# Joining the last weighted-sum burst of a cross-attention batch to the first burst of the next batch

## The chip, the cores and the metric

The kernel runs on one core of one Trainium2 chip. The metric is the device time of one execution in microseconds (us), as the median of several runs. The engines are named as the profile names them: PE (TensorE, matmuls; PEld is its weight loads), DVE (VectorE), ACT (ScalarE), POOL (GpSimd) and SP (SyncE, which issues most DMAs).

## The reference, cut to what matters

A decoder of two layers over 32 batches of 100 tokens with 256 features, all in float32. Each layer has self-attention, cross-attention over a context of 361 rows and a feed-forward part (layer 0: a scaled ternary matmul; layer 1: eight experts, of which each token takes one). A residual sum and a layer norm follow each of the three. The change is in cross-attention, which for each batch and each of 16 heads is:

```
scores = q @ k.T                     # 100 x 361; layer 0 adds -log(distance)*|scale|
attn   = softmax(scores, axis=-1)
out    = attn @ v                    # 100 x 16 per head
y      = out.reshape(100, 256) @ Wo + bo
x      = layernorm(x + y)
```

## The kernel before

**Tiling.** Heads are taken in four groups of four (`NG = 4`). For a cross group, PE makes the scores of four heads in four PSUM banks (`score`, L277, a tile of which there is one, shared with self-attention). DVE then reads each head once, adds the bias and finds the row maximum (L360, "reads" below); POOL subtracts the maximum (L364, "subtractions"); PE turns the 100x361 weights in three chunks of 120 or so (`turn`, L374, four transposes a chunk); ACT takes the exponential out of PSUM into the tile `pT` (L375); and PE multiplies by the values (`sums`, L389). The values carry 16 columns of ones beside each head's 16, so the sums give the softmax's denominator too. Four heads share the array, each in its own 32 columns. A float32 matmul is two matmul instructions, so the profile counts twice what the code issues.

**Bursts.** `sums` does nothing for group 0; for group 1 it does groups 0 and 1 in one burst (48 instructions in the profile), for groups 2 and 3 one group each (24). ACT copies a burst out to `av_x` (L391). `pT` has two buffers, the values `v_cross` two.

**The order of the work** is written out by hand. Work is planned in slots, five a batch, each with places -1 to 3; `run_slots` issues a slot so: the scores of the step two slots ahead and the first two reads; places -1 and 0; the other reads; then for the step one slot ahead the three chunks of transposes, with places 1, 2 and 3 after them; and last the bursts of the slot's own step. Every engine has one queue in this order. The batch at slot `start` has its cross groups at `start + 0, 1, 3, 4`; the self step of the batch four later has the slot between (`start + 2`). So in the steady state a period of five slots is, named by slot modulo 5:

- slot 0: scores of a self step; it ends when the scores of group 2 start
- slot 1: scores of group 2, the transposes of the self step, the burst of groups 0 and 1
- slot 2: scores of group 3, the transposes of group 2
- slot 3: scores of the next batch's group 0, transposes of group 3, the burst of group 2 and that of the self step
- slot 4: scores of the next batch's group 1, transposes of its group 0, the burst of group 3

For the self step, DVE reads the 16 heads' scores twice, for the maximum (L318, tile `mx_s`) and for the subtraction (L321, `pr_s`).

**The batch's tail** follows from `start + 5`: `add_share` on POOL (L296, tile `y_x`); `normalised` (four PE transposes, L287, tile `r_n_x`; DVE L289 and L291, `o_x`); `transpose_rows` (L242, `r_x_ox`); `residual` (PE L303, `r_o_x`; DVE L304, L85, L87; POOL L89 and L90, `rs_x`); the centring (DVE L94). Layer 0 goes on with the next norm's statistics (`mv_n`, POOL `rs_n`), `feed_forward_input` (DVE L579 to L581, tile `xn`) and its transposes (`r_x_n`). Layer 1 goes on with transposes for the router (`r_x_m`), the router's logits (`r_l`), and per four batches the ranking of tokens (`r_p`) and sending of rows. Self-attention has the same tail with tiles ending in `_s`.

Of the kernel before, what the change touches and what calls it, by code (L numbers as in the profile page):

```python
# [10 lines left out]
F32 = mybir.dt.float32  # L11
# [5 lines left out]
B, S, D, H, DH = 32, 100, 256, 16, 16  # L17
SK = 361
E = 8
P = 128  # L20
NC2 = D // P
NG = 4
KCH = [(0, 120), (120, 120), (240, 122)]
# [21 lines left out]
SHARED = ("l0s_wq", "l0s_wk", "l0s_wv", "l0x_wk", "l0x_wv", "l0x_wq", "l0s_wo", "l0x_wo")  # L45
# [5 lines left out]
def head(g, j):  # L51

    return 8 * (g // 2) + 2 * j + g % 2
# [11 lines left out]
def decoder_kernel(ctx: ExitStack, tc: tile.TileContext, a: dict, out: bass.AP):  # L65
    nc = tc.nc
# [6 lines left out]
    xnT = state.tile([P, NC2, B, S], F32, name="xnT")  # L73
# [22 lines left out]
    with ExitStack() as att:  # L96
        w1 = att.enter_context(tc.tile_pool(name="w1", bufs=1))
        w2 = att.enter_context(tc.tile_pool(name="w2", bufs=2))
# [5 lines left out]
        def bank(tag):  # L104
            return ps_r.tile([P, 512], F32, tag="r", name=f"r_{tag}")

        def split(t, n):
            return t.rearrange("p (n s) -> p n s", n=n)
# [18 lines left out]
        c = {}  # L127
# [12 lines left out]
        shared = const.tile([P, E, NC2 * D], F32, name="shared")  # L140
# [62 lines left out]
              ("s", 1): masked(1.0 / 16.0, None, "qm_s1"), ("x", 1): masked(0.25, c["l1x_bq"], "qm_x1")}  # L203

        def spread_value_bias(n):
            wide = c[n + "_wide"] = w1.tile([P, NC2, P], F32, tag=f"fold_{n[2]}", name=f"fold_{n}")
            nc.vector.tensor_copy(wide, c[n + "_bv"].unsqueeze(2).to_broadcast([P, NC2, P]))

        def fold_value_bias(n):
# [22 lines left out]
        def next_tile(tiles):  # L232
            tiles.append(tiles.pop(0))
            return tiles[-1]

        live = {}
# [37 lines left out]
        def score(dst, qz, kT, g, j):  # L274
            k, p = divmod(g, 2)
            rows = slice(32 * j, 32 * j + 32)
            nc.tensor.matmul(dst, lhsT=qz[rows, p, k, :], rhs=kT[rows, k, :], start=True, stop=True)  # L277

        def score_banks(tag):
            return ps_s.tile([P, NG, 512], F32, tag="s", name=f"sc_{tag}")  # L280

        def normalised(avs, tag):


            psn = bank(f"n_{tag}")[:S].rearrange("p (h r) -> p h r", r=32)
            for g in range(NG):
                nc.tensor.transpose(psn[:, g * NG:(g + 1) * NG, :].rearrange("p h r -> p (h r)"), avs[:, g, :], ident)  # L287
            rc = sm.tile([S, H], F32, tag="rc", name=f"rc_{tag}")
            nc.vector.reciprocal(rc, psn[:, :, DH])  # L289
            o = w2.tile([S, H, DH], F32, tag="o", name=f"o_{tag}")  # L290
            nc.vector.tensor_tensor(o, psn[:, :, :DH], rc.unsqueeze(2).to_broadcast([S, H, DH]), ALU.mult)  # L291
            return o

        def add_share(share, kind, b, tag):
            y = w2.tile([S, D], F32, tag=f"y_{kind}", name=f"y_{kind}{tag}")
            nc.gpsimd.tensor_tensor(y, xs[b], share[:S], ALU.add)  # L296
            return y
# [9 lines left out]
        def self_step(l, b):  # L307
# [34 lines left out]

            return Step(scores, turn, sums)

        def cross_step(l, b, g):

            t, tag = live[l, b], f"x{l}_{b}_{g}"

            def scores():
                sc = score_banks(tag)[:S, :, :SK]  # L350
                for j in range(NG):
                    score(sc[:, j, :], t["qz_x"], t["kT_x"], g, j)
                pr = t["pr_x", g] = next_tile(pr_cross)
                bias = zero if l else t["bias"]
                alone = b >= B - 4

                def centre(j):
                    def do():
                        mx = sm.tile([S, 1], F32, tag="mxx", name=f"mx_{tag}_{j}")
                        nc.vector.tensor_tensor_reduce(pr[:, j, :SK], sc[:, j, :], bias, 1.0, LOWEST, ALU.add, ALU.max, mx)  # L360
                        if alone and j == NG - 1:
                            nc.vector.tensor_scalar(pr[:, j, :SK], pr[:, j, :SK], mx, None, ALU.subtract)
                        else:
                            nc.gpsimd.tensor_tensor(pr[:, j, :SK], pr[:, j, :SK], mx.to_broadcast([S, SK]), ALU.subtract)  # L364
                    return do
                return [centre(j) for j in range(NG)]

            def turn(i):
                k0, n = KCH[i]
                if i == 0:  # L370
                    t["pT_x", g] = w2.tile([P, len(KCH), NG, S], F32, tag="pT", name=f"pT_{tag}")
                pt = split(bank(f"t_{tag}_{i}")[:, :NG * S], NG)
                for j in range(NG):
                    nc.tensor.transpose(pt[:n, j, :], t["pr_x", g][:, j, k0:k0 + n], ident[:S, :S])  # L374
                nc.scalar.activation(t["pT_x", g][:n, i], pt[:n], AF.Exp)  # L375

            def sums():

                if g == 0:
                    return  # L380
                groups = (0, 1) if g == 1 else (g,)
                if g == 1:
                    t["av_x"] = w2.tile([P, NG, S], F32, tag="avs_x", name=f"avs_{tag}")
                av = split(bank(f"a_{tag}")[:, :len(groups) * S], len(groups))
                for h, part in enumerate(groups):
                    for i, (k0, n) in enumerate(KCH):
                        n = min(n, SK - k0)
                        for j in range(NG):
                            nc.tensor.matmul(av[32 * j:32 * j + 32, h, :], lhsT=t["v_x"][:n, i, head(part, j), :],  # L389
                                             rhs=t["pT_x", part][:n, i, j, :], start=(i == 0), stop=(i == len(KCH) - 1))  # L390
                nc.scalar.copy(t["av_x"][:, groups[0]:g + 1, :], av)  # L391

            return Step(scores, turn, sums)

        plan, steps, bursts = {}, {}, {}

        def at(slot, place, do):
            plan.setdefault((slot, place), []).append(do)
# [68 lines left out]
        def starts(l, b):  # L467


            return LAYER[l] + SLOTS * b, LAYER[l] + (2 * b - 10 if b < 4 else SLOTS * (b - 4) + 2)  # L470
# [59 lines left out]
        def plan_batch(l, b):  # L530
            start, early = starts(l, b)
            t = live[l, b] = {}
            sx = f"l{l}x"
            tag = f"{l}_{b}"

            def keep(key, f):
                def do():
                    t[key] = f()
                return do
# [34 lines left out]
                nc.sync.dma_start(t["v_x"].rearrange("p i h r -> p (i h r)"), values_dram[b - AHEAD[0]])  # L574

            def feed_forward_input():
                xn = t["xn"] = w2.tile([S, D], F32, tag="xn", name=f"xn_{b}")
                mean, rs = t["ln_n"]
                nc.vector.scalar_tensor_tensor(xn, xs[b], mean, c["ffn_g"][:S], ALU.subtract, ALU.mult)  # L579
                nc.vector.scalar_tensor_tensor(xn, xn, rs, c["ffn_b"][:S], ALU.mult, ALU.add)  # L580
                nc.vector.tensor_reduce(absmax[:S, b:b + 1], xn, AX.X, ALU.max, apply_absolute_value=True)  # L581
# [43 lines left out]
            for g in range(NG):  # L625
                slot = start + (0, 1, 3, 4)[g]
                steps[slot] = cross_step(l, b, g)
                bursts.setdefault(slot, []).append(steps[slot].sums)
            at(start + 5, 0, keep("y_x", lambda: add_share(c[sx + "_bo"], "x", b, tag)))
            at(start + 5, 2, keep("o_x", lambda: normalised(t["av_x"], f"x{tag}")))  # L630
            at(start + 6, 0, keep("oT_x", lambda: transpose_rows(flat(t["o_x"]), "ox", tag)))
# [7 lines left out]
            else:  # L639
                at(start + 9, 0, keep("x3T", lambda: transpose_rows(xs[b], "m", tag)))  # L640
                first, n = group_of(b)
                r, steps_of_group = ROUTING[max(0, b - (B - 3))]
                at(start + r[0], r[1], router)
                if b == first + n - 1:
                    for do, (s, place) in zip((ranked, exponentials, ahead_of, counted, shares, rows_of), steps_of_group):
                        at(start + s, place, lambda do=do: do(first, n))
                    s, place = steps_of_group[-1]
# [11 lines left out]
        def group_of(b):  # L659

            if b >= B - 2:
                return b, 1
            first = b // GROUP * GROUP
            return first, min(GROUP, B - 2 - first)
# [145 lines left out]

        at(-16, 1, load_soon)
        at(-16, 1, lambda: spread_value_bias("l0s"))
        at(-16, 1, lambda: spread_value_bias("l0x"))
        at(SLOTS * B + 2, 0, lambda: spread_value_bias("l1x"))
        at(-12, 3, fold_first)
        at(-8, 1, lambda: fold_value_bias("l0x"))
        for l in range(2):
            for b in range(B):
                plan_batch(l, b)
            for b in range(0, B, 2):  # L820
                plan_pair(l, b)
# [196 lines left out]
```

## Time and profile before

| what | value |
|---|---|
| median of 3 runs | 1749.03 us (1747.58 to 1750.52) |
| the profiled execution | 1748.03 us |
| its span, first to last instruction | 1745.9 us |
| PE busy | 1681.2 us (96%) |
| DVE busy | 1291.6 us (74%) |
| POOL busy | 1096.9 us (63%) |
| ACT busy | 912.9 us (52%) |
| mean granted TensorE clock | 0.99 |

All times in the text are of the profiled execution. A line of a timeline has the start in us from the span's start, the time from the first start to the last end of the merged instructions, the engine, the line, the operation, output and inputs, the shapes and the count; in brackets the engine's idle time before and who ended it. Matmuls overlap, so the time that a group costs PE is the distance from its start to the start of the next group.

### The profile page before, as it was taken

To read this page: it belongs to the slowest core of one execution; us is meant where nothing else is said; L and a number is where in the kernel's file an instruction comes from. 1 tells how busy PE (TensorE), PEld (TensorE's weight loads), DVE (VectorE), ACT (ScalarE), POOL (GpSimd) and SP (SyncE) were. 2 spreads that over 40 slices of the span, in tenths; PEclk is the share of its full clock that TensorE was granted. 3 is DMA by queue.
4 is the path that set the end of the run, shared out by engine and by line. 5 is a ranking of instruction groups with operands and counts; after the bars stand their busy time and mean duration, and the time that the engine had idled before them with its cause. 6 is when DMAs were issued, how large, how long until landed. Compare 5 with 4: busy or idle time off the path is not lost. (4 is left out here: it accounts for less than half of the span.)

```text
span 1745.9 us, 52245 instructions
## 1 busy us (share of the span) xinstructions
PE 1681.2 (96%) x20801; PEld 1302.3 (75%) x20801; DVE 1291.6 (74%) x3784; ACT 912.9 (52%) x2252; POOL 1096.9 (63%) x1657
## 2 busy tenths in 40 slices
PE   8999999999999999999999999999999999999786
PEld 6777777777777777776777777777777777777575
DVE  5677777777777777777667787877777787777655
ACT  3455555555555555555445555555555555554354
POOL 1566666666566666666237667776767667675646
PEclk9999999999999999999999999999999999999888
DMA  4001322332233233310421132000100000100083
GB/s 160 14 22 30 81 76 54 85 81 64 70 81 84 48 82 81 76 30 22 160 63 55 55 103 65 19 20 19 28 19 21 18 22 26 37 27 18 18 257 113
DMA packets 64047, 104.90 MB, mean 60 GB/s; under 512 B 6107, under 2 KB 43485, under 8 KB 63678
## 3 DMA queue, kind: packets, MB, share of 16 engines
q1 hardware_dynamic: 59790, 94.44, 19.7%
q0 software_dynamic: 3584, 6.59, 1.2%
q8 instruction: 165, 2.70, 0.7%
q14 instruction: 76, 0.62, 0.1%
q10 hardware_dynamic: 432, 0.54, 0.1%
HBM read 61.32 MB, written 41.13 MB: 59 GB/s over the span
## 5 line engine op out<-in xcount | busy, mean ns | idle before, releaser
L364 POOL TENSOR_TENSOR pr<-pr,mx_x 100x361 f32<-100x361 f32 x992 | 766.3, 802 | 230.9 <-DVE mx_x L360 222.1
L375 ACT ACTIVATE pT_x<-r_t_x 120x400 f32<-120x400 f32 (+1 forms) x768 | 370.6, 503 | 271.2 <-PE r_t_x L374 269.2
L374 PEld LDWEIGHTS r_t_x<-ident,pr 100*120 100x120 f32 (+1 forms) x3072 | 313.7, 138 | 112.5 <-POOL pr L364 34.0
L374 PE MATMUL r_t_x<-ident,pr 100*120 100x100 f32 (+1 forms) x3072 | 380.7, 252 | 12.3 <-POOL pr L364 11.1
L360 DVE CUSTOM_DVE_ANT_0 pr<-sc_x,dist 100x361 f32<-100x361 f32 x512 | 244.7, 530 | 121.8 <-PE sc_x L277 97.7
L360 DVE CUSTOM_DVE_ANT_0 pr<-sc_x,zero 100x361 f32<-100x361 f32 x512 | 244.6, 530 | 76.7 <-PE sc_x L277 69.5
L277 PE MATMUL sc_x<-kT_x,qz_x 32*100 32x361 f32 x2048 | 221.8, 502 | 8.5 <-DVE mx_x L360 5.2
L89 POOL TENSOR_SCALAR rs_s<-mv_s 100x1 f32<-100x1 f32 x64 | 14.3, 224 | 289.7 <-DVE mv_s L87 261.6
L389 PE MATMUL r_a_x<-pT_x,v_cross 120*32 120x100 f32 (+1 forms) x6144 | 172.2, 252 | 0.0
L318 DVE TENSOR_REDUCE mx_s<-sc_s 100x16 f32<-100x1600 f32 x64 | 116.6, 1823 | 69.8 <-PE sc_s L277 69.8
L477 ACT ACTIVATE kT_x<-r_k,c_columns 128x361 f32<-128x361 f32 x128 | 72.0, 563 | 162.2 <-PE r_k L475 162.2
L389 PEld LDWEIGHTS r_a_x<-pT_x,v_cross 120*32 120x32 f32 (+1 forms) x6144 | 129.9, 110 | 24.1 <-ACT kT_s L424 2.1
L332 ACT ACTIVATE pT_s<-r_t_s 100x400 f32<-100x400 f32 x256 | 112.7, 504 | 30.2 <-PE r_t_s L331 27.6
L321 DVE TENSOR_TENSOR pr_s<-sc_s,mx_s 100x1600 f32<-100x1600 f32 x64 | 116.8, 1824 | 2.2
L331 PE MATMUL r_t_s<-ident,pr_s 100*100 100x100 f32 x1024 | 107.3, 251 | 0.3 <-DVE pr_s L321 0.3
L277 PEld LDWEIGHTS sc_x<-kT_x,qz_x 32*100 32x100 f32 x2048 | 68.3, 160 | 45.2 <-issue 13.8
L484 PE MATMUL r_v<-shared,ctx 128*120 128x256 f32 (+1 forms) x384 | 100.5, 384 | 0.0
L331 PEld LDWEIGHTS r_t_s<-ident,pr_s 100*100 100x100 f32 x1024 | 95.2, 130 | 5.5 <-ACT shared L486 0.6
L486 ACT COPY v_cross<-r_v 120x256 f32<-120x256 f32 x168 | 62.5, 372 | 58.0 <-PE r_v L484 58.0
L268 DVE SCALAR_TENSOR_TENSOR qz_x<-r_qx,qm_x_scale,qm_x_bias 128x400 f32<-128x400 f32 x64 | 37.6, 629 | 71.8 <-PE r_qx L257 71.8
L475 PE MATMUL r_k<-ctx,shared 128*128 128x361 f32 x256 | 88.6, 468 | 1.1 <-DMA ctx<-in_ctxT_dram 1.1
L475 PE MATMUL r_k<-ctx,c_l1x_wk 128*128 128x361 f32 x256 | 89.2, 470 | 0.0
(220 smaller groups left out, 2910.6 us busy)
## 6 DMA issues: line engine op xcount, KB each, us to landing
regions<-no_token SPq DMA_DIRECT2D x23, 1161.0 KB
ctx<-in_ctxT_dram SPq DMA_DIRECT2D x64, 361.0 KB
wb<-in_experts_dram SPq DMA_DIRECT2D x32, 257.0 KB
values_dram<-shared SPq DMA_DIRECT2D x8, 768.0 KB
v_cross<-values_dram SPq DMA_DIRECT2D x8, 768.0 KB
dist<-in_dist_dram SPq DMA_DIRECT2D x32, 141.0 KB
xb<-regions SPq DMA_DIRECT2D x32, 129.0 KB
x_all<-in_x_dram SPq DMA_DIRECT2D x32, 100.0 KB
```

The lines of the kernel that those rows point to most:

```text
L277: nc.tensor.matmul(dst, lhsT=qz[rows, p, k, :], rhs=kT[rows, k, :], start=True, stop=True)
L318: nc.vector.tensor_reduce(mx, sg, AX.X, ALU.max)
L321: nc.vector.tensor_tensor(pr, sg, mx.unsqueeze(3).to_broadcast([S, NG, NG, S]), ALU.subtract)
L331: nc.tensor.transpose(pt[:, j, :], t["pr_s"][:, j, g, :], ident[:S, :S])
L332: nc.scalar.activation(t["pT_s"][:, g], pt, AF.Exp)
L360: nc.vector.tensor_tensor_reduce(pr[:, j, :SK], sc[:, j, :], bias, 1.0, LOWEST, ALU.add, ALU.max, mx)
L364: nc.gpsimd.tensor_tensor(pr[:, j, :SK], pr[:, j, :SK], mx.to_broadcast([S, SK]), ALU.subtract)
L374: nc.tensor.transpose(pt[:n, j, :], t["pr_x", g][:, j, k0:k0 + n], ident[:S, :S])
L375: nc.scalar.activation(t["pT_x", g][:n, i], pt[:n], AF.Exp)
L389: nc.tensor.matmul(av[32 * j:32 * j + 32, h, :], lhsT=t["v_x"][:n, i, head(part, j), :], rhs=t["pT_x", part][:n, i, j, :], start=(i == 0), ...
L475: nc.tensor.matmul(ps, lhsT=c[sx + "_wk"][:, k, m * P:(m + 1) * P], rhs=t["ctx"][:, k, :], start=(k == 0), stop=(k == NC2 - 1))
L484: nc.tensor.matmul(ps, lhsT=ctx_b[:, k, k0:k0 + n], rhs=c[sx + "_wv"][:, k, :], start=(k == 0), stop=(k == NC2 - 1))
```

## The change

The sums of the last group (g = 3) are no longer issued in their own slot but with those of groups 0 and 1 of the next batch, two slots later, for all but the last three batches of a layer (`put_off`). That burst is then 72 instructions, with two copies by ACT. The whole tail of such a batch, routing included, moves by two slots. `pT` gets a third buffer, since the last group's turned weights live longer; for the room, the tile `xn` shares the buffers of `y_f`, and the spread value biases, used once each near the start of a layer, lie in parts of `xnT` and `shared` instead of tiles of their own.

```diff
         def spread_value_bias(n):
-            wide = c[n + "_wide"] = w1.tile([P, NC2, P], F32, tag=f"fold_{n[2]}", name=f"fold_{n}")
+            room = xnT[:, int(n[2] == "x"), :3, :] if n[1] == "0" else shared[:, SHARED.index("l0s_wo"), :]
+            room = room.rearrange("p b s -> p (b s)") if n[1] == "0" else room
+            wide = c[n + "_wide"] = room[:, :NC2 * P].rearrange("p (k s) -> p k s", k=NC2)
...
+        def put_off(b):
+            return b < B - 3
...
-                    t["pT_x", g] = w2.tile([P, len(KCH), NG, S], F32, tag="pT", name=f"pT_{tag}")
+                    t["pT_x", g] = w2.tile([P, len(KCH), NG, S], F32, tag="pT", name=f"pT_{tag}", bufs=3)
...
             def sums():
-                if g == 0:
+                if g == 0 or g == NG - 1 and put_off(b):
                     return
-                groups = (0, 1) if g == 1 else (g,)
+                parts = [(t, part) for part in ((0, 1) if g == 1 else (g,))]
                 if g == 1:
                     t["av_x"] = w2.tile([P, NG, S], F32, tag="avs_x", name=f"avs_{tag}")
-                av = split(bank(f"a_{tag}")[:, :len(groups) * S], len(groups))
-                for h, part in enumerate(groups):
+                    if b and put_off(b - 1):
+                        parts.insert(0, (live[l, b - 1], NG - 1))
+                av = split(bank(f"a_{tag}")[:, :len(parts) * S], len(parts))
+                for h, (u, part) in enumerate(parts):
                     for i, (k0, n) in enumerate(KCH):
                         n = min(n, SK - k0)
                         for j in range(NG):
-                            nc.tensor.matmul(av[32 * j:32 * j + 32, h, :], lhsT=t["v_x"][:n, i, head(part, j), :],
-                                             rhs=t["pT_x", part][:n, i, j, :], start=(i == 0), stop=(i == len(KCH) - 1))
-                nc.scalar.copy(t["av_x"][:, groups[0]:g + 1, :], av)
+                            nc.tensor.matmul(av[32 * j:32 * j + 32, h, :], lhsT=u["v_x"][:n, i, head(part, j), :],
+                                             rhs=u["pT_x", part][:n, i, j, :], start=(i == 0), stop=(i == len(KCH) - 1))
+                if len(parts) == 3:
+                    nc.scalar.copy(live[l, b - 1]["av_x"][:, NG - 1, :], av[:, 0, :])
+                first = 0 if g == 1 else g
+                nc.scalar.copy(t["av_x"][:, first:g + 1, :], av[:, len(parts) - (g + 1 - first):, :])
...
-                xn = t["xn"] = w2.tile([S, D], F32, tag="xn", name=f"xn_{b}")
+                xn = t["xn"] = w2.tile([S, D], F32, tag="y_f", name=f"xn_{b}")
...
                 steps[slot] = cross_step(l, b, g)
                 bursts.setdefault(slot, []).append(steps[slot].sums)
+            start += 2 * put_off(b)
             at(start + 5, 0, keep("y_x", lambda: add_share(c[sx + "_bo"], "x", b, tag)))
```

## The prediction

> **What bounds the kernel now.** I read the page first, then the timeline of PE in the steady parts of both layers, then the timelines of DVE and POOL in the same stretches. The page says that PE is nearly always at work and the others are not:
>
> ```profile
> PE 1681.2 (96%) x20801; PEld 1302.3 (75%) x20801; DVE 1291.6 (74%) x3784; ACT 912.9 (52%) x2252; POOL 1096.9 (63%) x1657
> ```
>
> A busy PE need not be at its peak, so I took the distances between starts. They repeat from period to period: layer 0 alternates between periods of 24.26 and 26.20 us, layer 1 (later batches) runs 23.97, 24.84, 24.42, 25.16 over four. Nearly every slot is the plain sum of its PE groups. First, what a burst costs (timeline, 600 to 624 us, layer 0):
>
> ```profile
> 604.73 0.51 PE L374 MATMUL r_t_x<-ident,pr 100*122 100x100 f32 x4
> ...
> 605.17 0.73 PE L389 MATMUL r_a_x<-pT_x,v_cross 120*32 120x100 f32 x24
> ...
> 611.37 0.72 PE L389 MATMUL r_a_x<-pT_x,v_cross 120*32 120x100 f32 x24
> ...
> 612.02 0.96 PE L277 MATMUL sc_s<-kT_s,qz_s 32*100 32x100 f32 x32
> ...
> 617.04 0.51 PE L374 MATMUL r_t_x<-ident,pr 100*122 100x100 f32 x4
> ...
> 617.48 0.86 PE L277 MATMUL sc_x<-kT_x,qz_x 32*100 32x361 f32 x8
> ...
> 620.15 1.25 PE L389 MATMUL r_a_x<-pT_x,v_cross 120*32 120x100 f32 x48
> ...
> 621.32 0.87 PE L277 MATMUL sc_x<-kT_x,qz_x 32*100 32x361 f32 x8
> ```
>
> Four transposes cost 0.44 up to a burst (604.73 to 605.17) and 0.44 up to scores (617.04 to 617.48). A burst of 24 up to scores costs 0.65 (611.37 to 612.02), one of 48 costs 1.17.
>
> Second, slot 0 of layer 1, where the self scores' two passes on DVE just fit:
>
> ```profile
> 1279.18 0.96 PE L277 MATMUL sc_s<-xT_s,qz_s 32*100 32x100 f32 x32
> ...
> 1280.21 1.83 DVE L318 TENSOR_REDUCE mx_s<-sc_s 100x16 f32<-100x1600 f32 x1 [1.59 <-PE sc_s L277]
> ...
> 1280.99 0.60 PE L287 MATMUL r_n_x<-ident,avs_x 128*100 128x128 f32 x4
> ...
> 1281.42 1.38 PE L475 MATMUL r_k<-ctx,c_l1x_wk 128*128 128x361 f32 x4
> ...
> 1282.07 1.82 DVE L321 TENSOR_TENSOR pr_s<-sc_s,mx_s 100x1600 f32<-100x1600 f32 x1
> ...
> 1283.95 0.87 PE L277 MATMUL sc_x<-kT_x,qz_x 32*100 32x361 f32 x8
> ```
>
> The next scores need the banks that `pr_s` reads. It ends at 1283.89, 4.71 after the self scores' start, and PE comes at 1283.95 from its own queue: no wait, and 0.05 us of room.
>
> Third, the way from DVE over POOL to the transposes of slot 2, in layer 0:
>
> ```profile
> 616.65 0.25 DVE L289 RECIPROCAL rc_x<-r_n_x 100x16 f32<-100x16 f32 x1
> ...
> 617.28 0.41 DVE L304 SCALAR_TENSOR_TENSOR y_s<-y_s,r_o_s 100x256 f32<-100x256 f32 x1
> ...
> 618.45 0.22 POOL L89 TENSOR_SCALAR rs_s<-mv_s 100x1 f32<-100x1 f32 x1 [5.51 <-DVE mv_s L87]
> ...
> 619.29 3.07 POOL L364 TENSOR_TENSOR pr<-pr,mx_x 100x361 f32<-100x361 f32 x4
> ```
>
> From the self scores (612.02) the fourth subtraction ends 10.34 later. In the period before (from 585.83) it ended 10.81 later, because `xn` held DVE when the self scores came, and there PE waited:
>
> ```profile
> 595.92 0.47 PE L374 MATMUL r_t_x<-ident,pr 100*120 100x100 f32 x3
> 596.69 0.30 PE L374 MATMUL r_t_x<-ident,pr 100*120 100x100 f32 x1 [0.30 <-POOL pr L364]
> ```
>
> The fourth transpose is 0.77 after the first where 0.26 is usual: 0.51 lost, in every second period of layer 0.
>
> **The change part by part.**
>
> *The burst.* It costs 0.65 in slot 4, and 1.17 - 0.65 = 0.52 more in slot 1: 0.13 saved a batch, for 29 batches in each of two layers 7.5 us, if PE alone were the bound. ACT makes three copies a batch as before. The 72-burst's inputs were made by ACT a slot earlier. The third `pT` buffer only lets the weights live on. The moved rooms are used once a layer, and `xn` and `y_f` belong to different layers; I cost both at nothing, with one DVE copy of `xn`'s kind (0.83) as what they would cost each layer if a wait showed.
>
> *The moved tail, on PE.* By distances of starts, the tail's groups are `r_n_x` 0.43, `r_x_ox` 0.17, `r_o_x` 0.87, `r_x_n` 0.17 (layer 0), `r_x_m` 0.23 and `r_l` 0.30 (layer 1). Two slots later means: slot 0 loses 0.43; slot 1 loses 0.34 in layer 0, 0.30 in layer 1, and gains 0.52; slot 2 loses 0.87 and gains 0.43; slot 3 gains 0.34 or 0.47; slot 4 loses 0.65 (and 0.23 in layer 1) and gains 0.87. The total is the 0.13 less. What counts is which slot has cover to lose.
>
> *Slot 4* keeps its cover: `r_o_x` stands where the burst was, so the self scores come 4.1 to 4.3 after the slot's own scores where the four reads need 3.57 (606.51 to 610.08).
>
> *Slot 0, layer 1.* PE's queue shrinks from 4.77 to 4.34, but the next scores cannot start before 4.71 + 0.05. `r_n_x`, which was free cover here, becomes work in slot 2: 0.43 lost a batch. Against it stand the 0.13, and waits in slot 2 that end because the burst of slot 1 is longer and `o_x` no longer stands before the reads: slot 2 is 6.89 where its groups add up to 6.64, every second batch, 0.15 a batch on average. In two of four later batches slot 0 was 5.24 and 5.09 (ranking matmuls; a subtraction behind a send), which the same 4.77 now swallows: 0.20 a batch, less 0.07 for the ranking matmuls, now in slot 2. Sum 0.43 - 0.13 - 0.15 - 0.20 + 0.07 = +0.02, times 19: +0.4. The first eight batches have periods of 21.95 and 22.83, no such extra waits, and a `y_x` on POOL amid the subtractions of a short slot 2 (0.74, up to 0.25 of it before PE every second batch): +0.13 to +0.38, I take 0.27: +2.2.
>
> *Slots 0 to 2, layer 0.* In DVE's queue after `pr_s`, the tail's `rc_x` and `o_x` (616.65 to 617.28, 0.63) give way to the centring and the next norm's statistics, which took 603.48 to 604.63, 1.15. All behind is 0.52 later: `y_s`, the statistics, POOL's `rs_s`, and the four reads and subtractions of slot 1, which queue behind them. `xn` leaves slot 4, so the self passes start on time in every period. The fourth subtraction then ends 10.34 + 0.52 = 10.86 after the self scores in every period. `xn` now runs in slot 1 after the reads, beside the last subtractions: the 26 subtractions that lay wholly beside its second pass (L580) took 0.97 on average, where 0.79 is usual, so 0.18 more: 11.04, and 0.05 to PE. PE comes earlier than before: 5.03 + 4.02 for slots 0 and 1 (5.46 - 0.43; 3.84 - 0.34 + 0.52), 0.80 for scores and 0.26 for three transposes make 10.1, or 10.5 with the query transposes of every second batch (0.40). Waits of 0.98 and 0.58, 1.56 a pair, where 0.51 a pair is today. Less twice 0.13: +0.79 a pair, +0.39 a batch. Some 26 batches run in this steady state: +10.1. Without the 0.18 it is +5.5, with two subtractions so slowed +15.
>
> The Trainium skill (SBUF — State Buffer, "Who interferes with whom") says that a VectorE instruction with two SBUF inputs contends with a GpSimd read, and that the shared port is an exclusive lock whose loser blocks. By that a subtraction could stand still for all of L580's 0.82 instead of 0.18, and 26 times 0.64 would add 17 us. The trace has 0.18, and I go by it.
>
> The later reads of slot 2 (DVE is free at about 11.6 instead of 10.1) and `y_x` on POOL between them put its fourth subtraction at about 16.0; slot 3's fourth transpose comes at 16.0 or later. I count nothing, and 0.3 every second batch (4 us) for the upper end.
>
> *Sum.* 10.1 + 0.4 + 2.2 = +12.7 on the profiled 1748.03; that execution is 1.0 below the median, so the forecast is 1749.0 + 12.7 = 1762. About 0.2% (3.5 us) can be told from no change.
>
> **The rivals.**
>
> *PE is the bound everywhere in layer 0 (not slower).* If reads and subtractions of slot 1 end by 10.1 after the self scores, 0.9 before my chain, layer 0 loses all its waits: 26 times (0.13 + 0.26) = -10.1, and with layer 1's +2.6 the time is 1741.5. For it: PE is 96% busy, and POOL idles between. Against: those waits are on latency, with rows for each link, and one is already there today. Chance 0.13.
>
> *The chain is 0.2 to 0.4 shorter* (no port contention, and layer 1 keeps its relief in slot 2): +5.5 - 3, 1751.5. Chance 0.10.
>
> *The backlog spreads:* `xn` and `y_x` make slot 3 wait as well, and two subtractions are slowed: +15 + 4 + 5 in layer 1, 1773. Against: both slots 2 and 3 have long periods every second batch. Chance 0.17.
>
> That the change does not do what it says I rule out: in the program's order the 36 matmuls stand together and slot 4 has none.
>
> **How the numbers follow.** The forecast has 0.60. Faster is most of the first rival, 0.12; within 0.2% most of the second, 0.10; slower the rest, 0.78. The range leaves out the bulk of the first rival and the worst of the third: 1745 to 1775; the forecast's own range is 1755 to 1768.
>
> **What would show it.** Right: in layer 1 slot 0 stays at 4.77 with PE waiting about 0.4 for `pr_s`; in layer 0 the fourth transpose of slot 2 waits for POOL in every period, 0.6 to 1.0; the waits of PE for POOL's `pr` grow by 10 us or more; burst distances are 1.69 for 72. Wrong: layer 0 periods at or below 24.1 and 25.5, no POOL wait in slot 2, or DVE reads in slot 1 starting under 6.6 after the self scores.

## The result, and the profile after

The changed kernel takes 1764.63 us (median of 6 runs, 1760.37 to 1766.01); the kernel before, beside it on the same chip, 1749.76 (6 runs). The ratio is 1.0089, 95% interval [1.0076, 1.0102]: slower by 0.9%. Its profiled execution took 1762.92, with a span of 1761.0, 15.1 more than before. In the changed kernel lines moved: L360, L364, L374, L389, L277, L321 and L580 of before are L366, L370, L380, L398, L279, L323 and L592.

The two groups of PE that wait more, on the page before. The last columns are PE's idle time just before the group and what ended most of it:

```profile
L374 PE MATMUL r_t_x<-ident,pr 100*120 100x100 f32 (+1 forms) x3072 | 380.7, 252 | 12.3 <-POOL pr L364 11.1
...
L277 PE MATMUL sc_x<-kT_x,qz_x 32*100 32x361 f32 x2048 | 221.8, 502 | 8.5 <-DVE mx_x L360 5.2
```

The page after, first the line of the engines and then the same two groups:

```profile
PE 1678.6 (95%) x20801; PEld 1304.5 (74%) x20801; DVE 1295.0 (74%) x3784; ACT 908.7 (52%) x2252; POOL 1088.7 (62%) x1657
...
L380 PE MATMUL r_t_x<-ident,pr 100*120 100x100 f32 (+1 forms) x3072 | 381.6, 252 | 19.8 <-POOL pr L370 18.7
...
L279 PE MATMUL sc_x<-kT_x,qz_x 32*100 32x361 f32 x2048 | 221.7, 502 | 18.0 <-DVE pr_s L323 12.1
```

PE does the same 20801 matmul instructions in 2.6 us less busy time, and yet ends 15 later. What grew are waits: those in front of the transposes, most of them for POOL, from 12.3 to 19.8, and those in front of the scores, most of them for DVE, from 8.5 to 18.0.

Layer 0, one period of the changed kernel (timeline, 589 to 601 us):

```profile
589.71 0.96 PE L279 MATMUL sc_s<-kT_s,qz_s 32*100 32x100 f32 x32
...
592.60 1.82 DVE L323 TENSOR_TENSOR pr_s<-sc_s,mx_s 100x1600 f32<-100x1600 f32 x1
...
594.35 0.41 DVE L94 TENSOR_SCALAR x_all<-y_x,mv_x,rs_x 100x256 f32<-100x256 f32 x1
...
594.79 0.43 DVE L85 BATCH_NORM_STATS2 st_n<-x_all 100x6 f32<-100x256 f32 x1
...
595.35 0.39 DVE L306 SCALAR_TENSOR_TENSOR y_s<-y_s,r_o_s 100x256 f32<-100x256 f32 x1
...
596.33 0.50 DVE L366 CUSTOM_DVE_ANT_0 pr<-sc_x,dist 100x361 f32<-100x361 f32 x1
...
597.06 1.76 PE L398 MATMUL r_a_x<-pT_x,v_cross 120*32 120x100 f32 x72
...
597.32 3.25 POOL L370 TENSOR_TENSOR pr<-pr,mx_x 100x361 f32<-100x361 f32 x4
...
598.75 0.87 PE L279 MATMUL sc_x<-kT_x,qz_x 32*100 32x361 f32 x8
...
599.55 0.47 PE L380 MATMUL r_t_x<-ident,pr 100*120 100x100 f32 x3
...
600.63 0.30 PE L380 MATMUL r_t_x<-ident,pr 100*120 100x100 f32 x1 [0.60 <-POOL pr L370]
```

The centring and the statistics stand between `pr_s` and `y_s`; the reads follow, then POOL's four subtractions (597.32 to 600.57); three transposes are through, and the fourth starts 1.08 after the first, where 0.26 to 0.31 is usual. The burst of 72 (597.06 to 598.75) has its 1.69. In the other of the two periods that alternate, the wait is there too, but shorter (timeline, 626 to 627.5 us):

```profile
626.26 0.42 PE L380 MATMUL r_t_x<-ident,pr 100*120 100x100 f32 x3
626.94 0.30 PE L380 MATMUL r_t_x<-ident,pr 100*120 100x100 f32 x1 [0.26 <-POOL pr L370]
```

Layer 1, slot 0 (timeline, 1286 to 1292 us):

```profile
1286.77 0.96 PE L279 MATMUL sc_s<-xT_s,qz_s 32*100 32x100 f32 x32
...
1289.66 1.82 DVE L323 TENSOR_TENSOR pr_s<-sc_s,mx_s 100x1600 f32<-100x1600 f32 x1
...
1290.69 0.51 PE L380 MATMUL r_t_x<-ident,pr 100*122 100x100 f32 x4
...
1291.54 0.87 PE L279 MATMUL sc_x<-kT_x,qz_x 32*100 32x361 f32 x8 [0.35 <-DVE pr_s L323]
```

Slot 0 is again 4.77 (1286.77 to 1291.54), but PE's queue is through earlier and PE waits for `pr_s`. PE's waits, summed over the span (us in total, times, longest), show how often, after and then before:

```profile
PE r_t_x L380 <- POOL pr L370: 18.7, 43, 0.8
PE sc_x L279 <- DVE pr_s L323: 12.1, 28, 1.8
```

```profile
PE sc_x L277 <- DVE pr_s L321: 3.2, 2, 1.8
```

Two long waits (1.4 and 1.8) for `pr_s` are in both kernels. The other 26 are new, 8.9 in all and 0.34 each. By starts it is a little more: four transposes cost 0.44, so in the lines above PE could have come at 1291.13, and it came 0.41 later. That is the `r_n_x` (0.43) that was taken out of this slot.

By stretches, from starts of self scores in the two timelines (profiled executions, us):

| stretch | before | after | difference | predicted |
|---|---|---|---|---|
| layer 0 up to its last period | 737.2 | 742.4 | +5.2 | +10.1 |
| last period of layer 0, feed-forward and start of layer 1 | 164.8 | 164.1 | -0.8 | 0 |
| layer 1, first eight periods | 182.3 | 182.2 | -0.1 | +2.2 |
| layer 1, next 19 periods | 464.9 | 472.8 | +7.9 | +0.4 |
| the rest (experts, end) | 196.7 | 199.5 | +2.8 | 0 |

The differences are taken before rounding. Two rows hold a difference of the granted clock. The first is that of the first eight periods of layer 1. Slot 1 of the first of them has the same groups of PE in both kernels; before, then after (busy time of each engine, then the granted clock):

```profile
906.90:913.80 6.90, 6.90 (x87) 6.04 (x87) 3.08 (x10) 2.57 (x6) 3.03 (x4) 0.75 0.01 2
```

```profile
911.35:916.57 5.22, 5.21 (x84) 4.36 (x84) 3.08 (x10) 2.25 (x6) 3.03 (x4) 1.00 0.02 5
```

In before's profiled execution PE ran at half clock for 3.4 us from 908.1, and the slot took 6.89. In e9_layer0_norm_later, e11_norm_later_short and e12_five_alone, whose layer 1 is that of before, it took 5.22 at full clock, and the eight periods took 180.5 to 180.6. So the change costs +1.6 there, and the -0.1 of the table is a slow place in before's execution.

The second is the last row. Two stretches of the end, 15 us each, after and before:

```profile
1662.00:1677.00 15.00, 4.84 (x22) 3.87 (x20) 5.79 (x34) 1.82 (x3) 5.19 (x9) 0.50 0.17 42
```

```profile
1650.00:1665.00 15.00, 3.46 (x15) 2.53 (x15) 5.36 (x33) 2.19 (x4) 4.27 (x7) 0.50 0.27 67
```

PE runs at half clock in both, while it has little to do. The whole half-clock stretch was 30.7 us long after (from 1654.7) and 20.5 before (from 1648.7). The run e4_cover below, whose order at the end is the changed kernel's, had 20.5 and spent 196.9 on the rest, as before does; so the 2.8 are not there in every execution of that order.

### The profile page after: what moved, and what is told of

It reads as the page before. It is cut to its first block, busy times and chain, and to the rows that moved or that the text cites. A ratio compares the mean times of both kernels' runs of the same rounds, so it can differ in the third digit from the quotient of the medians.

```text
span 1761.0 us, 52136 instructions
## 1 busy us (share of the span) xinstructions
PE 1678.6 (95%) x20801; PEld 1304.5 (74%) x20801; DVE 1295.0 (74%) x3784; ACT 908.7 (52%) x2252; POOL 1088.7 (62%) x1657
## 5 line engine op out<-in xcount | busy, mean ns | idle before, releaser
L370 POOL TENSOR_TENSOR pr<-pr,mx_x 100x361 f32<-100x361 f32 x992 | 765.8, 799 | 287.4 <-DVE mx_x L366 284.1
L380 PE MATMUL r_t_x<-ident,pr 100*120 100x100 f32 (+1 forms) x3072 | 381.6, 252 | 19.8 <-POOL pr L370 18.7
L380 PEld LDWEIGHTS r_t_x<-ident,pr 100*120 100x120 f32 (+1 forms) x3072 | 317.1, 138 | 104.1 <-POOL pr L370 33.6
L366 DVE CUSTOM_DVE_ANT_0 pr<-sc_x,zero 100x361 f32<-100x361 f32 x512 | 243.9, 528 | 115.3 <-PE sc_x L279 83.0
L366 DVE CUSTOM_DVE_ANT_0 pr<-sc_x,dist 100x361 f32<-100x361 f32 x512 | 243.4, 528 | 94.8 <-PE sc_x L279 91.1
L279 PE MATMUL sc_x<-kT_x,qz_x 32*100 32x361 f32 x2048 | 221.7, 502 | 18.0 <-DVE pr_s L323 12.1
L398 PE MATMUL r_a_x<-pT_x,v_cross 120*32 120x100 f32 (+1 forms) x6144 | 161.2, 252 | 0.0
L398 PEld LDWEIGHTS r_a_x<-pT_x,v_cross 120*32 120x32 f32 (+1 forms) x6144 | 131.5, 110 | 17.7 <-ACT pT_x L381 1.1
L323 DVE TENSOR_TENSOR pr_s<-sc_s,mx_s 100x1600 f32<-100x1600 f32 x64 | 116.8, 1825 | 2.2
L279 PEld LDWEIGHTS sc_x<-kT_x,qz_x 32*100 32x100 f32 x2048 | 68.2, 159 | 56.8 <-issue 20.3
L366 DVE DVE_READ_ACCUMULATOR2_ANT mx_x<- 100x1 f32 x1024 | 84.5, 83 | 0.0
```

The lines of the kernel that those rows point to most:

```text
L323: nc.vector.tensor_tensor(pr, sg, mx.unsqueeze(3).to_broadcast([S, NG, NG, S]), ALU.subtract)
L398: nc.tensor.matmul(av[32 * j:32 * j + 32, h, :], lhsT=u["v_x"][:n, i, head(part, j), :], rhs=u["pT_x", part][:n, i, j, :], start=(i == 0), ...
```

## The experiments

What they left, in us from the start of a slot's scores to the start of the next slot's, in the profiled executions. Layer 0, the two periods that alternate:

| kernel | slots 0 to 4, first period | second period | pair |
|---|---|---|---|
| before | 5.46 3.84 5.46 5.93 5.51 | 5.46 3.84 6.64 4.20 4.11 | 50.46 |
| changed | 5.04 4.00 5.34 6.27 5.66 | 5.04 4.00 6.70 4.55 4.31 | 50.90 |
| e2_tail | 5.05 3.50 5.84 6.27 6.36 | 5.04 3.50 7.19 4.55 4.96 | 52.25 |
| e5_norm_later | 5.22 4.00 4.52 6.10 5.66 | 5.22 4.00 6.26 4.38 4.31 | 49.66 |
| e8_layer0_five | 5.54 4.19 4.94 6.10 4.81 | 5.46 4.18 6.64 4.37 3.62 | 49.86 |
| e12_five_alone | 5.46 3.67 5.34 6.10 5.51 | 5.46 3.67 6.69 4.37 4.11 | 50.39 |

Layer 1, the sum of four later periods (after which they repeat): before 98.41, changed 100.20, e2_tail 101.96, e3_five 99.81, e6_routing_five 99.12, e7_y_x_early 99.94. Of these four, by slots:

| kernel | slot 0 | slot 1 | slot 2 | slot 3 |
|---|---|---|---|---|
| before | 4.77 4.77 5.24 5.09 | 3.98 5.75 3.98 5.75 | 6.89 4.94 6.87 4.94 | 4.20 5.25 4.20 5.25 |
| changed | 4.77 4.77 4.77 4.77 | 4.18 5.92 4.62 5.92 | 6.22 4.52 6.84 4.52 | 4.73 5.78 4.99 6.34 |

Diffs are against the changed kernel. The comparisons are with runs of the kernel before on the same chip, whose medians lay between 1748.7 and 1750.2.

**The rooms and the buffer alone (e1_rooms).**

```diff
         def put_off(b):
-            return b < B - 3
+            return False
```

> The changed kernel with nothing put off: the third buffer for turned weights and the moved rooms alone. My theory (the moved tail costs, the burst itself saves) expects the time of before, 1749 us, within 2. The rival that another placement in SBUF or the third buffer costs the time expects most of the change's +15 us here, 1760 or more.

Measured: 1747.56, ratio 0.9993 [0.9984, 1.0003]. The third buffer and the shared rooms cost nothing that can be told; all of the result is the moved work.

**The tail moved, the bursts left apart (e2_tail).**

```diff
-                if g == 0 or g == NG - 1 and put_off(b):
+                if g == 0:
...
-                    if b and put_off(b - 1):
-                        parts.insert(0, (live[l, b - 1], NG - 1))
```

> The tail of each batch moved by two slots, but every burst left where it was. My theory: the tail is what costs. In layer 0 the chain to slot 2's transposes sets the time up to there, so the 0.52 us that slot 1 loses against the change turns into waiting, and slot 4 has its 0.65 burst again: +0.65 a batch over the change, 17 us in 26 batches; in layer 1 0.13 for the burst and about 0.2 of new waiting in slot 2, 8 us; together 1790 us (1775 to 1795). The rival that the joined burst itself costs (values and weights of two batches in one burst, two copies behind it) expects the tail's move to be free: 1748 to 1753.

Measured: 1793.92, ratio 1.026 [1.0243, 1.0277]. It is the moved tail that costs; the join takes back 29 of its 45 us. By the table it is worth 0.68 a batch in layer 0 and 0.44 in layer 1, far more than the 0.13 that it saves PE: it clears slot 4 of 0.65 to 0.70, and what it adds to slot 1 (0.50) comes out of slot 2, where PE waits for POOL (5.84 to 5.34, 7.19 to 6.70).

**The tail a whole period later (e3_five).**

```diff
-            start += 2 * put_off(b)
+            start += 5 * put_off(b)
...
                 wait = 2 * (b == B - 2)
+                wait += 2 * put_off(b)
```

> The bursts joined as in the change, but the tail put off by five slots, a whole period, so that each of its steps stands in the same slot of the period as before the change; only the feed-forward input and its transposes go two further, from slots 4 and 1 to slots 1 and 3, since slot 4 is now too short for them. My theory: slot 0 has its cover again (4.77 in layer 1 without waiting, 5.46 in layer 0), slot 4 is bound by the score reads at 3.62, slot 1 is 0.52 longer, which ends the waits of slot 2. Layer 0: periods of about 24.28 and 25.56, 8 us less than before in 26 batches; layer 1: 0.14 less a batch, 3.5 us: 1738 us (1733 to 1745). The rival that the joined burst itself costs expects 1760 or more; the rival that any delay of the tail costs expects more than the change, over 1764.

Measured: 1764.65, ratio 1.0096 [1.0079, 1.0113]; a miss by 27. Layer 0 came as expected: its last period starts 9.3 earlier than before's. That period, with the feed-forward behind it, was then 7.3 longer (123.1 for 115.8), layer 1 up to its last period 13.7 longer (709.9 for 696.2) and the rest 4.6. In layer 1 the place of the burst in slot 4 stayed empty, and the self scores now came before the reads had emptied their banks. What PE's self scores waited for (us, times):

```profile
  DVE mx_x L366: 16.9, 15
```

In the changed kernel, where `r_o_x` fills that place, this is 4.0, and in before 2.1. These waits are of the size of layer 1's loss, but no run took them away. The clock has a part too: the profiled execution has five stretches at half clock between 815 and 1266 us, 20.5 us in all, and the mean clock of all four executions is 0.982 or 0.983, where the changed kernel's have 0.987 to 0.990. How the miss divides between the two is open.

**Free cover (e4_cover).** Four transposes of a constant are added to slot 0 of 25 periods of layer 1, where `r_n_x` has gone; their result is not used.

```diff
+            def cover():
+                ps = bank(f"cover_{tag}")
+                for k in range(NG):
+                    nc.tensor.transpose(ps[:, k * P:(k + 1) * P], ident, ident)
+            if l and 3 < b < B - 3:
+                at(start + 5, 2, cover)
```

> The change with four 128x128 transposes of a constant added in slot 0 of 25 batches of layer 1 (their result is not used): 0.43 us of PE work each. My theory says that PE waits 0.43 there for DVE's second pass over the self scores, so they cost nothing: 1764 to 1767 us. If PE were the bound in that slot they would cost 25 times 0.43: 1775 us.

Measured: 1761.82, ratio 1.0082 [1.0065, 1.0099]. The timeline of the same slot as above:

```profile
1286.44 0.96 PE L279 MATMUL sc_s<-xT_s,qz_s 32*100 32x100 f32 x32
...
1288.25 0.60 PE L644 MATMUL r_cover<-ident 128*128 128x128 f32 x4
1288.69 1.38 PE L487 MATMUL r_k<-ctx,c_l1x_wk 128*128 128x361 f32 x4
...
1291.21 0.87 PE L279 MATMUL sc_x<-kT_x,qz_x 32*100 32x361 f32 x8
```

The transposes take 0.44 of PE (1288.25 to 1288.69), the slot is still 4.77, and the wait is gone: 25 times 0.44, 11 us of matmuls, for nothing (the 19 later periods take 472.8 in both kernels). So the forecast's step was right that `r_n_x` was free where it stood.

**The norm behind the reads (e5_norm_later).**

```diff
-            at(start + 8, 1, lambda: centre_and_scale(xs[b], t["y_x"], t["ln_x"]))
+            later = int(l == 0 and put_off(b))
+            at(start + 8 + later, 1, lambda: centre_and_scale(xs[b], t["y_x"], t["ln_x"]))
...
-                at(start + 8, 2, keep("ln_n", lambda: layer_norm_scale(sm, xs[b], 0.001, "n", f"n_{b}")))
-                at(start + 9 + wait, 3, feed_forward_input)
-                at(start + 11 + wait, 3, lambda: transpose_rows(t["xn"], "n", tag, dst=xnT[:, :, b, :]))
+                at(start + 8 + later, 2, keep("ln_n", lambda: layer_norm_scale(sm, xs[b], 0.001, "n", f"n_{b}")))
+                at(start + 9 + wait + 2 * later, 1 if later else 3, feed_forward_input)
+                at(start + 11 + wait + 2 * later, 3, lambda: transpose_rows(t["xn"], "n", tag, dst=xnT[:, :, b, :]))
```

> The changed kernel, but in layer 0 the centring of the batch's result and the next norm's statistics (the 1.00 us of DVE work that stands between the self passes and y_s in slot 0) move from slot 0 to slot 1, behind the four reads; the feed-forward input and its transposes move later with them, so that the order of dependence stays. My theory: PE's waits of 0.49 and 0.81 a pair in slot 2 of layer 0 come from this 1.00 alone, since the four reads and POOL's subtractions queue behind it. Then these waits go: some 12 pairs by 1.3 = -16 at most, less what the statistics then delay in slot 1 and 2; I expect 1749 (1745 to 1755), and a fourth subtraction that ends about 9.9 instead of 10.86 after the self scores. Rival (the waits are set by POOL's own pace or by PE's earlier arrival, not by the work ahead of the reads): the time stays at 1762 to 1766 and the waits in slot 2 stay above 0.4.

Measured: 1751.6, ratio 1.0011 [1.0001, 1.0022], 13 less than the changed kernel. One period of layer 0 (timeline, 553 to 565 us):

```profile
553.78 0.96 PE L279 MATMUL sc_s<-kT_s,qz_s 32*100 32x100 f32 x32
...
560.65 3.08 POOL L370 TENSOR_TENSOR pr<-pr,mx_x 100x361 f32<-100x361 f32 x4
...
561.86 0.48 DVE L94 TENSOR_SCALAR x_all<-y_x,mv_x,rs_x 100x256 f32<-100x256 f32 x1
...
564.22 0.51 PE L380 MATMUL r_t_x<-ident,pr 100*120 100x100 f32 x4
```

The fourth subtraction ends at 563.73, 9.95 after the self scores (10.86 in the changed kernel), and the four transposes stand in one piece with no wait. The pair is 1.24 shorter: slot 2 loses its waits of 0.82 and 0.44, and the rest is matmuls that changed slots. The edit moves two things, the centring with the statistics and `xn`: the subtractions start 0.74 earlier after the self scores (7.61 to 6.87), and beside no `xn` they take 3.08 instead of 3.25. Together the two are the chain from DVE over POOL, and it is the cause of layer 0's loss.

**Routing in its old slots (e6_routing_five).** Layer 1's transposes for the router, the logits, the ranking and the sends come three slots later still.

```diff
             else:
+                start += 3 * put_off(b)
                 at(start + 9, 0, keep("x3T", lambda: transpose_rows(xs[b], "m", tag)))
```

> The changed kernel, but layer 1's router part (the normalised input's transposes, the router's matmuls, the ranking, the sends) is put off by five slots in all instead of two, so that it falls into the same slot of the period as in the kernel before, one batch later. The joined bursts and the rest of the moved tail stay. My theory: the 8 us that layer 1 lost beyond the forecast come from routing steps in the wrong slots (the ahead copies on DVE in slot 0, logits and sends among the subtractions of slot 3). Then they come back for the most part: 1755 (1752 to 1759), with layer 1's later periods at 24.6 on average instead of 25.05. Rival (the loss is the cover taken from slot 0, or y_x among the subtractions of slot 2 and 3): 1763 to 1766, periods unchanged.

Measured: 1756.43, ratio 1.0041 [1.0027, 1.0056]. The 19 later periods of layer 1 take 468.0, against 472.8 in the changed kernel and 464.9 before; its first eight are 2.0 shorter. So 4.8 of the 7.9 were routing steps in slots where they stand in the way. One such place in the changed kernel (timeline, 1341 to 1346 us), eight short DVE steps of routing in front of the reads:

```profile
1341.89 0.14 DVE L707 COPY ahead<-sofar 100x8 f32<-100x8 f32 x1
...
1343.28 0.17 DVE L708 TENSOR_TENSOR sofar<-sofar,hot 100x8 f32<-100x8 f32 x1
1343.37 0.53 DVE L366 CUSTOM_DVE_ANT_0 pr<-sc_x,zero 100x361 f32<-100x361 f32 x1
...
1345.32 0.87 PE L279 MATMUL sc_x<-kT_x,qz_x 32*100 32x361 f32 x8 [0.37 <-DVE mx_x L366]
```

They hold DVE from 1341.89 to 1343.37, the reads come late, and PE waits 0.37 for the banks. The other 3.1, 0.16 a period, stay; their cause is not shown.

**`y_x` in its old slot (e7_y_x_early).**

```diff
-            start += 2 * put_off(b)
             at(start + 5, 0, keep("y_x", lambda: add_share(c[sx + "_bo"], "x", b, tag)))
+            start += 2 * put_off(b)
```

> The changed kernel, but the residual sum y_x on POOL stays in the slot where the kernel before has it (slot 0), in both layers: as the last group's output share is joined later now, this is only the part of the sum that does not need it. All else stays. My theory gives y_x among the subtractions of slots 2 and 3 a small part of layer 1's surplus, about 0.1 a batch: 1761 (1759 to 1764). Rival (y_x is the cause of the waits in layer 1's slot 3): 1756 to 1758, with slot 3 back to 4.2 and 5.25. A second rival (y_x does not matter): 1764.6.

Measured: 1759.39 (1758.52 to 1766.38), ratio 1.0055 [1.0037, 1.0073]. The timeline shows a small part, as expected: one period in four is 25.44 for 25.68, and the 19 later periods are 1.0 shorter in all. The profiled execution is the slowest of the four: its first seven periods took 6.5 more than the changed kernel's, with half clock for 6.8 us from 16.0 and for 3.4 from 80.8, while the later periods of layer 0 are equal to 0.01. So the 5 us between the medians are not explained by `y_x`. Much of it may be the clock: where the mean clock is 0.990 in both kernels, an execution took 1758.52 here and 1760.37 in the changed kernel.

**Layer 0 alone, a period later (e8_layer0_five).**

```diff
-        def put_off(b):
-            return b < B - 3
+        def put_off(l, b):
+            return l == 0 and b < B - 8
...
-            start += 2 * put_off(b)
+            start += 5 * put_off(l, b)
...
                 wait = 2 * (b == B - 2)
+                wait += 2 * put_off(l, b)
```

> The change only in layer 0, with the tail put off by five slots (a whole period, so each step falls into the slot it had before) and the feed-forward's input and transposes two slots further, and only for the batches up to the ninth from the end, so that nothing is put off across the end of the layer. Layer 1 is as in the kernel before. My theory: the joined burst saves what it was meant to save where the tail keeps its place in the period; the run with all tails five slots later had periods of 24.28 and 25.58 in layer 0 against 24.26 and 26.20, that is -0.31 a batch; 22 steady batches give -7: 1742 (1740 to 1745). Rival (putting off has a price where it ends, or layer 1 starts worse): 1749 or more.

Measured: 1740.92, ratio 0.9958 [0.9941, 0.9975]. Faster than both kernels, as expected.

**Layer 0 alone, the norm behind the reads (e9_layer0_norm_later).** The diff of e5_norm_later with `put_off(l, b)` as `l == 0 and b < B - 3`.

> The joined bursts only in layer 0, with the tail two slots later and the next norm's centring and statistics in slot 1 behind the reads (as in the run that moved them), and layer 1 as in the kernel before. My theory: layer 0 then has periods of 24.16 and 25.50 against 24.26 and 26.20 before, and the rows up to the end of layer 0 took 713.5 there against 721.6 before, 8.1 less; layer 1 gives and takes nothing. I expect 1742 (1738 to 1744), as fast as or faster than the run with five slots. Rival (the joined burst gains only where layer 1 has it as well, or the end of layer 0 costs more): 1747 or more.

Measured: 1740.9, ratio 0.9952 [0.9938, 0.9965].

**Both repairs (e10_both).** The diffs of e5_norm_later and e6_routing_five together.

> The changed kernel with both repairs: in layer 0 the centring and the next norm's statistics behind the reads of slot 1, in layer 1 the router part five slots later in all. My theory takes the two costs as separate: the first was worth 13.0 and the second 8.2 against the changed kernel's 1764.6, so both give 1743 (1740 to 1746). Rival (the two repairs give back partly the same loss, such as the tail of the run): 1748 or more.

Measured: 1746.19 (10 runs), ratio 0.9978 [0.9967, 0.9989]. The two are separate costs for the most part: 18.4 of the 21.2 expected, between the two theories' figures. Its periods are those of the two runs; by the profiled executions the missing 3 lie in the last period of layer 0 (119.5 for e5_norm_later's 117.4) and at the end of the run (198.9 for 197.7, with the longest stretch at half clock, 30.7).

**The same without the last eight batches (e11_norm_later_short).**

```diff
-            return l == 0 and b < B - 3
+            return l == 0 and b < B - 8
```

(against e9_layer0_norm_later)

> As the run with joined bursts in layer 0 alone, the norm's statistics behind the reads, but with nothing put off for the last eight batches of the layer. There the last stretch of layer 0 (from the self scores of its last regular period on) took 119.5 against 115.8 before, 3.7 more; the five batches that lose their gain cost 5 x 0.40 = 2.0. My theory: 1739 (1737 to 1741). Rival (the last stretch is longer for another reason): 1741 to 1744.

Measured: 1739.22 (1737.65 to 1740.3), ratio 0.9944 [0.9929, 0.996]. The last period of layer 0 is 115.8 again. This is the lowest median, 0.56% below the kernel before; its interval overlaps those of e8_layer0_five and e9_layer0_norm_later, so it is not shown to be the fastest of the three.

**The move without the join (e12_five_alone).** Against e8_layer0_five, the diff of e2_tail, with its `put_off(l, b)`.

> As the run with the tail five slots later in layer 0 (up to the ninth batch from its end), but the bursts stay apart, in the slots of the kernel before: the move alone, without the joined burst. Both together saved 0.32 a batch (periods of 24.28 and 25.58 against 24.26 and 26.20). My theory by the distances: 0.13 of that is the joined burst, the rest comes from the norm's input leaving the slot in which the self scores come; then the move alone saves 0.19 in each of 22 batches, 4: the time is 1744.5 (1743 to 1746.5). First rival (the joined burst saves it all): 1749. Second rival (the move saves it all): 1741.

Measured: 1747.65, ratio 0.9991 [0.9981, 1.0002]. The first rival is nearer: the move alone saves 0.07 a pair, and the join 0.53 a pair, 0.27 a batch. Of this, slots 4, 0 and 1 give 0.08 together (slot 4 is 1.19 shorter a pair, slots 0 and 1 are 1.11 longer); the other 0.45 come out of slot 2 (5.34 to 4.94, 6.69 to 6.64): there PE waits for POOL once a pair (0.18 of idle in e12_five_alone, almost none in e8_layer0_five), and a longer burst in slot 1 fills the wait.

## Why the prediction was right, and where its sum was off

Predicted were 1762.0 and slower; measured 1764.6. The mechanism in layer 0 is shown (by taking the chain's DVE work away, e5_norm_later), and so is the lost cover in slot 0 of layer 1 (by putting cover back at no cost, e4_cover). That the sum came out near is luck, since errors cancel: layer 0 was forecast 5.7 too long (4.9 and 0.8) and layer 1's first eight periods 0.6, while 7.5 were missing in its later periods. The granted clock adds 2.8 at the end of one profiled execution and takes 1.7 off in layer 1, where the other had its half clock.

*The burst.* 72 instructions take 1.69, as said. But 0.13 a batch is only what PE saves. The distances between kernels with and without the join are 0.68 and 0.27 a batch in layer 0, because the burst moved to where PE waits anyway. The forecast had this inside its slots, not as a term: slots 0 and 1 were forecast at 5.03 and 4.02 and are 5.04 and 4.00.

*The chain in layer 0.* Forecast: shift 0.52, contention 0.18, fourth subtraction at 11.04, waits 0.98 and 0.58, +0.39 a batch. Measured: the subtractions start 0.34 later after the self scores (7.27 to 7.61), contention 0.18 (3.07 to 3.25), fourth subtraction at 10.86, waits 0.82 and 0.44 (slot 2 against e5_norm_later's), +0.22 a batch. The mis-sized term is the 1.15 for centring and statistics. It was a duration from first start to last end, 603.48 to 604.63, of an instance beside POOL's subtractions; in slot 0 POOL has none, the centring took 0.41 for 0.48, and up to the start of `y_s` the three took 1.00. The 26 subtractions beside the second pass over `xn` (L592) took 0.96 on average against 0.79, as forecast from before's 26. In both kernels these lie beside the end of the first pass as well, so "wholly beside its second pass" is too much. Two signs failed with the size: POOL's waits grew from 11.1 to 18.7 and not "by 10 us or more", and the shorter of the two waits is under the "0.6 to 1.0".

*Slot 0 of layer 1* was right: 4.77 in every later period, with the 0.43 of `r_n_x` lost to `pr_s`.

*The rest of layer 1.* For the first eight periods the forecast was +2.2, and at full clock it is +1.6. (Of before's eight, only four have the lengths 21.95 and 22.83 that the forecast names; the others lie between 22.41 and 24.53.) The later periods were wrong: +0.02 each came to +0.41 (7.9 over 19). By the table of slots the credits came true: slot 0 is 4.77 in all four periods, and slot 2 fell to 6.22, near the 6.20 that 6.89 - 0.87 + 0.43 less the wait of 0.25 gives. What had no term is on the other side: the routing's own steps, moved by two slots, make slot 1 (4.62 for 4.18), slot 2 (6.84 for 6.22) and slot 3 (4.99 for 4.73, 6.34 for 5.78) longer in two of the four periods, those with the ranking and the sends, by their matmuls and by new waits behind DVE and POOL (0.24 of the 6.34 is `y_x`, by e7_y_x_early). The forecast counted their matmuls (0.07) and not the DVE queue in front of the reads. e6_routing_five puts 4.8 of the 7.9 there. The forecast's 0.3 for slot 3 stood in its upper end alone.

*The end* had no term; the 2.8 go with the longer stretch at half clock in this execution.

*The shared port.* The forecast went by the 0.18 of the trace, and 0.18 is what it was. Its other figure, 17 us, has the subtraction as the loser for the whole of the pass. In the traces the subtraction starts first (0.42 before the second pass in the kernel before, 0.35 in the changed one), and it is the pass that loses more (last section), so that figure has the wrong engine wait.

*The rivals.* That PE is the bound in layer 0 (1741.5) is refuted: with the chain shortened the waits go and the time falls by 13, with the chain in place they are there in every period. The shorter chain (1751.5) was half right: the chain is 0.18 shorter than forecast, though not for want of contention, and layer 1 gave the gain back. The backlog (1773) is there in slot 3 of layer 1 only in small.

## What to carry to other kernels

Work on an engine that is 95% busy is still free where that engine waits for another, and moving it away turns it into time: before moving a group, look in both slots for the wait that it covers, and cost it by the slots' lengths and not by its own. Moving a whole chain by less than a period moves every step past every other queue; keeping it in its place in the period, or moving the one step that stands in front of the next engine's input, turned 0.9% slower into 0.4 to 0.6% faster, where it was kept to layer 0. Test the two places of a change apart: here layer 0 had a gain to give, and layer 1 gave none in the versions tried. And look at the granted clock in each stretch before reading a difference of 2 us out of two profiles.

## What was not expected of the hardware

*DVE beside POOL.* The centring on DVE, from SBUF to SBUF, before and then after (ns, least, median, most):

```profile
L94 DVE TENSOR_SCALAR x_all<-y_s,mv_s,rs_s x64: 400/626/871, 39.1 to 1579.3; 100x256 f32<-100x256 f32 x64
L94 DVE TENSOR_SCALAR x_all<-y_x,mv_x,rs_x x64: 405/481/1474, 98.6 to 1652.2; 100x256 f32<-100x256 f32 x64
```

```profile
L94 DVE TENSOR_SCALAR x_all<-y_s,mv_s,rs_s x64: 397/880/930, 39.4 to 1591.6; 100x256 f32<-100x256 f32 x64
L94 DVE TENSOR_SCALAR x_all<-y_x,mv_x,rs_x x64: 402/406/1473, 111.6 to 1665.6; 100x256 f32<-100x256 f32 x64
```

The change moves `x_all<-y_x` out from beside POOL's subtractions (0.48 to 0.41). `x_all<-y_s` mostly lies beside them in both kernels, and goes from 0.63 to 0.88. Clear of POOL's two-input steps nearly all of these take 0.40 to 0.47, and beside them anything from 0.40 to 1.00, with the same shape: at the worst more than twice as long. The passes over `xn` take 0.48 clear of POOL; in the changed kernel's layer 0 they take 1.00 and 0.89, and the fourth subtraction beside them 0.96 for 0.79. So DVE loses more there than POOL does. The Trainium skill (SBUF — State Buffer, "Who interferes with whom") has the two engines share a port pair as an exclusive lock, and has the order of issue decide which of them blocks. The rows agree in that the second pass, which starts 0.35 after the subtraction, loses most; the subtraction's own 0.17 they do not settle, because it overlaps the first pass as well.

*The clock at the end.* The stretch at half clock after the layers was 20.5 us long in seven of the fourteen profiled executions, 23.9 in two, 27.3 in two and 30.7 in three. All six kernels whose layer 1 is as before had 20.5, and of the eight whose layer 1 is changed only e4_cover had it. With one profiled execution of each, that is a hint of a link and no more; what sets the length stays open.
